# A transformer block with expert routing on one core: new places for every sequence in the hand-made order, and the first weights in another order on two queues

## The chip, the core and the metric

The kernel runs on one core of a Trainium2 chip. A core has TensorE (PE, matrix products; its weight loads are listed as PEld), VectorE (DVE), ScalarE (ACT), GpSimd (POOL) and SyncE (SP, which here only issues DMAs). Each engine takes its instructions in a fixed order; semaphores make one wait for another. The metric is the device time of one execution in microseconds (us); the time before is the median of three runs. A line such as L556 is a line of the kernel file of before. In the changed file the same lines stand lower down by up to 56.

## The reference

Sixteen sequences of 256 tokens with 256 features pass through an attention block with 16 heads of 64, and then through a layer of 8 experts. Each expert takes the 512 tokens that have the highest gate value for it, over all 4096 tokens. All arithmetic is float32. Cut to what matters:

```python
shift = silu(t) @ W_ada.T + b_ada
h = ln(x, ln1_g, ln1_b) + shift
qkv = (h @ Wqkv.T).reshape(b, n, 3, H, HD)
q = ln(qkv[:, :, 0].transpose(0, 2, 1, 3), qn_g, qn_b)
k = ln(qkv[:, :, 1].transpose(0, 2, 1, 3), kn_g, kn_b)
v = qkv[:, :, 2].transpose(0, 2, 1, 3)
attn = softmax(einsum('bhnd,bhmd->bhnm', q, k) / sqrt(HD))
o = einsum('bhnm,bhmd->bhnd', attn, v).transpose(0, 2, 1, 3).reshape(b, n, H * HD)
x = x + o @ Wout.T
tok = x.reshape(-1, d)
gate = softmax(tok @ Wgate.T)
vals, idx = top_k(gate.T, tok.shape[0] // E)
g = ln(tok[idx.T.reshape(-1)], mlp_g, mlp_b).reshape(-1, E, d)
y = gelu(einsum('ked,ehd->keh', g, fc1s) + b1s)
y = einsum('keh,edh->ked', y, fc2s) + b2s
tok = tok.at[idx.T.reshape(-1)].add((y * vals.T[..., None]).reshape(-1, d))
```

## The kernel before

**The work of a sequence.** `First` normalises the two 128-token tiles of x, transposes them (L524) and evicts them with the shift's bias into `hT`. Twelve `Group`s project: groups 0 and 1 are queries, 2 and 3 keys, 4 and 5 values, each for two token tiles t, with 512 columns of the weights `wq`. A query or key group is a chain over the engines: `matmul` (L556, PE), `square` (L569, ACT), `stats` (L573, DVE), `power` (L82, POOL: the inverse root), `scale` (L589, DVE), `transposes` (L598, PE), `evict` (L610, ACT). The mean over a head is taken out by centring the weights once, in place, at the beginning (`center`, L478 to L480). Value groups are only copied (L565) into a tile with the tag `v`.

Four `Quad`s d of four heads each do the attention. A quad has two halves i, and each half two heads j: `scores` (L631, PE), `maxima` (L638, DVE), `exps` (L647, ACT), `invert` (L654, DVE), `normalise` (L658, POOL), `transposes` (L667, PE), `copy` (L675 on DVE or L677 on ACT), `product` (L685, PE), and for the quad as a whole `evict` (L697, DVE) into `oT`. Scores and transposed probabilities share four PSUM tiles with the tag `sc`, projections and most transposes three with `mm`, and the products of a quad, the output projection and the gate share a single one, `po`. Scores use 64 rows of the array for each head, products 64 columns, and all else the full array. `Tail` projects the output (L709), adds x, stores the token, normalises it, and computes the gate (L731, L742).

**Routing and experts.** After the gates of sequences 0 to 14 stand (`Gates`, `Routing.turn`), a search of 30 steps finds each expert's threshold: `compare` (L826, DVE), `count_over` (L856 and L857, PE, result `pc`), `either` and `decide` (DVE). Its steps are strewn among the work of sequence 15. Then the places of the chosen tokens are turned (L912), the token lists of the first experts come from one-hot products (L985, `pls`), tokens are gathered, and sixteen jobs (eight experts, two halves) run up (L1032) and down (L1048) projections. The first matmuls of the experts stand inside the planned order; the rest is a plain loop after it.

**What sets the order.** Every step of the attention is entered in a list with a number, its place, and the list is sorted by place. Engines get their instructions in this order, so a place decides only what stands ahead of what. A steady sequence b has the places of `STEADY` plus b x `PERIOD`. `START` overrides them for the first sequences, `END` for the last ones; `SHIFT` and `CENTER` place the shift and the weights' centring, `GATES`, `TURN`, `SEARCH`, `PLACE`, `LIST`, `UP`, `DOWN` the routing and the first experts. `quad` in the tables has for (d, i) scores, inversion and product, for (d, i, j) the five steps of a head, and `out` has the quads' evictions.

**The first loads.** Before the planned order, SP issues x of sequence 0 (`load_x(0)`), the weights `wa` of the shift, then the groups of `wq` in the order 0, 2, 4, x of sequence 1, 1, 3, 5, and last the output weights `wo`. ACT issues only the small vectors. x of a later sequence is issued by SP 20 places ahead of the sequence's first statistics of tile 0.

Of the kernel before, what the change touches and what calls it, by code (L numbers as in the profile page):

```python
# [18 lines left out]
P = 128  # L19
# [15 lines left out]
GW = 512  # L35
# [8 lines left out]
def kernel(  # L44
# [35 lines left out]
    def rsqrt(dst, src):  # L80
# [59 lines left out]
    PERIOD = 55.74  # L140
    STEADY = dict(
        first=((-86.48, -78.84, -74.84), (-85.13, -84.23, -75.17), (-73.21, -72.54)),
        group={
            (0, 0): (-51.60, -49.66, -48.99, -47.86, -45.60, -40.27, -37.29),
            (0, 1): (-49.89, -47.94, -45.00, -43.96, -42.22, -32.07, -31.41),
            (1, 0): (-24.39, -22.45, -21.77, -20.73, -18.77, -16.60, -15.29),
            (1, 1): (-26.11, -24.16, -23.49, -22.45, -20.71, -11.67, -10.68),
            (2, 0): (-39.83, -37.89, -37.22, -36.18, -34.31, -31.64, -30.60),
            (2, 1): (-38.12, -34.68, -33.12, -32.08, -28.64, -21.80, -20.95),
            (3, 0): (-7.64, -4.23, -3.56, -1.89, 2.62, 3.70, 6.68),  # L150
            (3, 1): (-9.35, -7.41, -6.74, -3.55, -1.19, 9.31, 9.98),
            (4, 0): (-53.91, -51.13),
            (4, 1): (-42.15, -39.94),
            (5, 0): (-11.07, -8.97),
            (5, 1): (-4.61, -2.66),
        },
        quad={
            (0, 0): (0.00, 4.89, 9.75),
            (0, 0, 0): (1.42, 3.71, 5.16, 7.57, 8.23),
            (0, 0, 1): (2.02, 2.81, 6.07, 8.00, 8.67),  # L160
            (0, 1): (-1.04, 3.21, 12.60),
            (0, 1, 0): (0.23, 1.01, 6.97, 8.87, 9.54),
            (0, 1, 1): (0.83, 1.91, 3.48, 8.44, 9.26),
            (1, 0): (10.73, 16.50, 25.41),
            (1, 0, 0): (12.00, 12.78, 17.68, 19.77, 22.02),
            (1, 0, 1): (14.11, 14.89, 16.77, 19.33, 21.66),
            (1, 1): (11.77, 21.34, 28.26),
            (1, 1, 0): (15.91, 19.26, 22.51, 24.97, 25.74),
            (1, 1, 1): (14.71, 20.16, 21.61, 24.53, 25.95),
            (2, 0): (26.39, 30.55, 40.23),  # L170
            (2, 0, 0): (28.29, 29.37, 30.82, 33.50, 35.62),
            (2, 0, 1): (27.69, 28.47, 31.73, 34.37, 35.60),
            (2, 1): (27.43, 36.22, 43.08),
            (2, 1, 0): (29.48, 30.27, 37.58, 39.57, 40.24),
            (2, 1, 1): (28.88, 33.89, 36.67, 38.70, 39.86),
            (3, 0): (41.21, 45.50, 53.71),
            (3, 0, 0): (42.48, 43.26, 46.67, 50.69, 51.36),
            (3, 0, 1): (43.08, 44.16, 45.77, 50.25, 50.92),
            (3, 1): (42.25, 50.11, 56.57),
            (3, 1, 0): (44.90, 45.87, 51.28, 53.28, 53.94),  # L180
            (3, 1, 1): (45.58, 48.93, 50.38, 52.84, 53.67),
        },
        out=(15.31, 30.96, 44.30, 59.03),
        tail=((75.94, 79.63, 83.54, 87.30, 84.99, 86.37, 88.80, 89.54), (90.54, 94.23, 95.33, 101.91, 95.74, 99.41, 105.55, 106.29)),
# [3 lines left out]
            first=((-103.767, -95.871, -91.909), (-97.063, -91.499, -84.828), (-64.982, -60.069)),  # L188
            group={
                (0, 0): (-56.803, -54.747, -51.852, -46.726, -46.286, -40.948, -38.071),  # L190
                (0, 1): (-55.655, -51.889, -46.959, -45.652, -42.360, -35.597, -33.112),
                (1, 0): (-26.197, -24.462, -20.588, -19.209, -14.535, -13.716, -13.269),
                (1, 1): (-32.516, -25.059, -24.852, -21.979, -18.889, -16.671, -15.729),
                (2, 0): (-47.233, -46.547, -44.993, -44.096, -39.234, -33.671, -28.238),
                (2, 1): (-45.275, -40.554, -40.280, -39.778, -36.553, -34.586, -30.446),
                (3, 0): (-12.610, -11.185, -8.404, -8.124, -5.996, 0.834, 3.448),
                (3, 1): (-13.363, -12.739, -11.605, -8.322, -7.543, 0.483, 2.162),
                (4, 0): (-58.243, -54.205),
                (4, 1): (-38.500, -37.978),
                (5, 0): (-9.805, -0.465),  # L200
                (5, 1): (-0.114, 0.811),
            },
            quad={
                (0, 0): (-23.919, -5.908, 12.730),
                (0, 0, 0): (-18.292, -15.414, 1.499, 3.539, 11.030),
                (0, 0, 1): (-14.279, -11.333, -0.174, 4.332, 10.767),
                (0, 1): (-19.036, -1.502, 16.728),
                (0, 1, 0): (-15.547, -8.095, 3.988, 5.433, 14.399),
                (0, 1, 1): (-14.367, -13.775, 4.740, 9.194, 12.898),
                (1, 0): (-9.076, 3.092, 27.287),  # L210
                (1, 0, 0): (-6.911, -0.007, 10.749, 23.221, 26.164),
                (1, 0, 1): (-7.145, 1.038, 18.097, 23.303, 26.927),
                (1, 1): (-5.313, 10.835, 30.672),
                (1, 1, 0): (-5.048, 3.942, 10.903, 21.602, 24.260),
                (1, 1, 1): (-2.237, 6.984, 16.287, 26.090, 28.843),
                (2, 0): (14.616, 29.160, 50.712),
                (2, 0, 0): (18.721, 20.212, 39.985, 46.847, 48.427),
                (2, 0, 1): (17.079, 22.439, 35.099, 36.543, 39.030),
                (2, 1): (14.417, 20.717, 53.224),
                (2, 1, 0): (19.017, 20.432, 39.871, 41.557, 46.931),  # L220
                (2, 1, 1): (16.395, 19.203, 33.057, 36.198, 43.625),
                (3, 0): (28.358, 39.182, 56.816),
                (3, 0, 0): (33.283, 33.907, 42.060, 47.233, 48.706),
                (3, 0, 1): (30.676, 31.677, 45.808, 50.648, 52.914),
                (3, 1): (29.455, 40.685, 56.950),
                (3, 1, 0): (34.034, 35.650, 42.042, 47.065, 52.989),
                (3, 1, 1): (31.817, 31.879, 48.481, 49.433, 55.328),
            },
            out=(21.163, 46.372, 54.377, 59.310),
        ),  # L230
        1: dict(
            first=((-48.940, -38.543, -32.714), (-52.735, -35.719, -31.997), (-29.207, -15.966)),
            group={
                (0, 0): (2.354, 2.737, 3.370, 7.803, 9.249, 18.355, 19.310),
                (0, 1): (4.127, 4.691, 6.834, 9.818, 13.020, 18.898, 22.093),
                (1, 0): (24.336, 28.826, 29.227, 31.339, 32.252, 41.371, 43.504),
                (1, 1): (21.258, 24.606, 28.113, 28.269, 30.764, 34.230, 38.901),
# [7 lines left out]
                (5, 1): (31.404, 35.141),  # L245
            },
        ),
        2: dict(
            first=((6.450, 29.164, 41.308), (24.474, 31.729, 34.174), (50.589, 52.650)),
        ),  # L250
    }
# [1018 lines left out]
```

## Time and profile before

| | us |
|---|---|
| median of 3 runs (1200.65 to 1202.83) | 1201.21 |
| the profiled execution | 1200.95 |
| its span, first to last instruction | 1199.2 |
| L556 projections, 768 records | 357.5 busy, 603 ns each |
| L685 products, 1024 records | 137.7 busy, 391 ns each |
| L667 transposes of the probabilities, 1024 | 136.7 busy, 274 ns each |
| L631 scores, 1024 records | 128.7 busy, 390 ns each |
| L658 normalise on POOL, 512 | 239.9 busy, 489 ns each |
| L647 exps on ACT, 512 | 236.5 busy, 477 ns each |

The first three rows are one execution seen from outside and from inside: what lies between span and time is outside the program's instructions. In a group's row, the busy time is the union of its instructions, and the ns are the length of one. Matmuls are pipelined, so the length of a record is longer than the distance from one start to the next; for what a record costs, starts are to be compared. A float32 matmul leaves two records, a transpose one.

The attention's weights are in within the first 20 us. The expert stage, after about 960 us, keeps PE filled.

### The profile page before, as it was taken

How to read it: one execution, taken by the hardware profiler on the slowest of the kernel's cores; microseconds unless marked ns; L12 is line 12 of the kernel's file. 1: busy time of each engine (PE TensorE's matmuls, PEld its weight loads, DVE VectorE, ACT ScalarE, POOL GpSimd, SP SyncE). 2: the span in 40 equal slices, each digit the busy share in tenths (PEclk: the TensorE clock that was granted, in tenths of full speed). 3: DMA queues.
4: the chain of work that ended last, by engine and by line, in shares of the span. 5: the costliest groups of instructions: out<-in, count | busy, mean ns of one | idle time of the engine just before them, and what ended most of it. 6: DMA issues, size and time to landing. Idle time of an engine off the chain costs nothing. (4 is left out here: it accounts for less than half of the span.)

```text
span 1199.2 us, 19564 instructions
## 1 busy us (share of the span) xinstructions
PE 1169.5 (98%) x6814; PEld 814.2 (68%) x6814; DVE 765.0 (64%) x2274; ACT 618.8 (52%) x1701; POOL 593.5 (49%) x820
## 2 busy tenths in 40 slices
PE   6999999999999999999999999999999899999996
PEld 3566666666675756666666666667755788888885
DVE  7666666657566657666666766665488567865541
ACT  2765565655556655555565655565575233333331
POOL 4564555555454555655555555555574333333332
PEclk9999999999999999999999999999999899999999
DMA  5000000000000000000001000000110366666661
GB/s 186 1 1 5 22 6 23 9 19 10 19 14 14 14 14 27 1 27 5 24 5 31 10 10 10 18 14 15 35 67 2 110 185 184 185 183 183 184 185 23
DMA packets 46738, 62.40 MB, mean 52 GB/s; under 512 B 3888, under 2 KB 39984, under 8 KB 46640
## 3 DMA queue, kind: packets, MB, share of 16 engines
q1 hardware_dynamic: 39808, 52.70, 13.1%
q0 software_dynamic: 6144, 8.39, 3.9%
q8 instruction: 54, 0.88, 0.3%
q14 instruction: 44, 0.36, 0.1%
q10 hardware_dynamic: 688, 0.06, 0.0%
HBM read 48.56 MB, written 12.58 MB: 51 GB/s over the span
## 5 line engine op out<-in xcount | busy, mean ns | idle before, releaser
L658 POOL TENSOR_SCALAR pr<-pr,sums 128x256 f32<-128x256 f32 x512 | 239.9, 489 | 265.1 <-DVE sums L654 252.0
L556 PE MATMUL pm<-wq,hT 128*128 128x512 f32 x768 | 357.5, 603 | 4.2 <-DMA wq<-in_wqkvT 2.7
L647 ACT ACTIVATE pr<-sc,nmax 128x256 f32<-128x256 f32 x512 | 236.5, 477 | 155.3 <-DVE nmax L638 154.8
L82 POOL TENSOR_TENSOR ss<-ss,neghalf 128x8 f32<-128x8 f32 x128 | 210.7, 1650 | 107.0 <-DVE ss L577 98.6
L556 PEld LDWEIGHTS pm<-wq,hT 128*128 128x128 f32 x768 | 137.6, 192 | 145.2 <-issue 134.0
L638 DVE TENSOR_REDUCE nmax<-sc 128x2 f32<-128x512 f32 x256 | 164.8, 681 | 43.4 <-PE sc L631 42.8
L573 DVE TENSOR_REDUCE ss<-sq 128x8 f32<-128x512 f32 x128 | 87.4, 683 | 107.1 <-ACT sq L569 107.0
L667 PEld LDWEIGHTS pp<-ident,pr 128*128 128x128 f32 x1024 | 118.3, 143 | 29.5 <-issue 18.3
L685 PE MATMUL po<-prT,v 128*64 128x256 f32 x1024 | 137.7, 391 | 0.1
L667 PE MATMUL pp<-ident,pr 128*128 128x128 f32 x1024 | 136.7, 274 | 0.0
L631 PE MATMUL sc<-kT,qT 64*128 64x256 f32 x1024 | 128.7, 390 | 0.0
L569 ACT ACTIVATE sq<-pm 128x512 f32<-128x512 f32 x128 | 77.1, 603 | 91.0 <-PE pm L556 89.4
L709 PE MATMUL pw<-wo,oT 128*128 128x256 f32 x512 | 119.1, 386 | 0.0
L1048 PE MATMUL py<-w,hid 128*128 128x256 f32 x512 | 119.0, 385 | 0.0
L1032 PE MATMUL ph<-xT,w 128*128 128x256 f32 x512 | 118.2, 383 | 0.0
L631 PEld LDWEIGHTS sc<-kT,qT 64*128 64x128 f32 x1024 | 93.4, 186 | 34.3 <-issue 23.6
L1058 POOL DMA_INDIRECT out<-y,idx x32 | 51.5, 1611 | 122.2 <-DVE y L1055 61.3
L709 PEld LDWEIGHTS pw<-wo,oT 128*128 128x128 f32 x512 | 96.7, 194 | 14.3 <-issue 1.2
L647 ACT ACTIVATION_READ_ACCUMULATOR pr<-sc,nmax 128x1 f32 x512 | 106.2, 207 | 0.0
L675 DVE COPY prT<-pp 128x512 f32<-128x512 f32 x112 | 76.9, 687 | 45.0 <-PE pp L667 44.7
L1048 PEld LDWEIGHTS py<-w,hid 128*128 128x128 f32 x512 | 96.1, 192 | 13.6
L1039 ACT ACTIVATE hid<-ph,vec 128x256 f32<-128x256 f32 x128 | 60.3, 474 | 85.8 <-PE ph L1032 74.4
(129 smaller groups left out, 1311.8 us busy)
## 6 DMA issues: line engine op xcount, KB each, us to landing
w<-in_fc2T SPq DMA_DIRECT2D x16, 1024.0 KB
w<-in_fc1T SPq DMA_DIRECT2D x16, 1024.0 KB
xs<-in_x SPq DMA_DIRECT2D x16, 256.0 KB
out<-tok SPq DMA_DIRECT2D x32, 128.0 KB
xn_dram<-tn SPq DMA_DIRECT2D x32, 128.0 KB
wq<-in_wqkvT SPq DMA_DIRECT2D x6, 512.0 KB
b<-in_b2s SPq DMA_DIRECT2D x16, 128.0 KB
wo<-in_woutT SPq DMA_DIRECT2D x1, 1024.0 KB
```

Source lines behind the costliest of these rows:

```text
L82: nc.gpsimd.tensor_tensor(dst, src, neghalf[:, : src.shape[1]], ALU.pow)
L556: nc.tensor.matmul(self.pm, hTs[self.b][:, c, bass.ts(self.t, P)], wq[:, c, bass.ts(self.g, GW)], start=(c == 0), stop=(c == DC - 1),)
L573: nc.vector.tensor_reduce(self.ss[:, 0, :], self.sq.rearrange("p (h d) -> p h d", d=HD), AX.X, ALU.add,)
L631: nc.tensor.matmul(self.sc[i, j][:, t, :], qTs[self.b][rows, hp, bass.ts(t, P)], kTs[self.b][rows, hp, :], start=True, stop=True,)
L638: nc.vector.tensor_reduce(self.nmax[i, j], self.sc[i, j], AX.X, ALU.max, negate=True)
L647: nc.scalar.activation(self.pr[i, j][:, t, :], self.sc[i, j][:, t, :], AF.Exp, bias=self.nmax[i, j][:, t : t + 1], scale=1.0, accum_out=se ...
L658: nc.gpsimd.tensor_scalar(self.pr[i, j][:, t, :], self.pr[i, j][:, t, :], self.sums[i][:, 1, j, t : t + 1], 1.0, ALU.mult, ALU.mult,)
L667: nc.tensor.transpose(self.pp[i, j][:, c, bass.ts(t, P)], self.pr[i, j][:, t, bass.ts(c, P)], ident,)
L685: nc.tensor.matmul(self.po[j * HD : (j + 1) * HD, i, :], vs[self.b][:, c, bass.ts(4 * self.d + 2 * i + j, HD)], self.prT[i, j][:, c, :], s ...
L709: nc.tensor.matmul(self.pw, oTs[self.b][:, hp, bass.ts(self.t, P)], wo[:, hp, :], start=(hp == 0), stop=(hp == HP - 1),)
L1032: nc.tensor.matmul(self.ph[f], self.w1[:, c, bass.ts(f, P)], self.xT[:, c, :], start=(c == 0), stop=(c == DC - 1),)
L1048: nc.tensor.matmul(self.py[i], self.hid[:, f, bass.ts(i, P)], self.w2[:, f, :], start=(f == 0), stop=(f == FC - 1),)
```

## The change

Three things change. The tables of places are new throughout: `STEADY` and `PERIOD`, `START`, which now also covers the quads of sequence 1 and the groups of sequence 2, `END`, and all the routing tables. No step is added or left out on PE, DVE, ACT or POOL. The first weights come in the order 4, 0, 2 on SP, and x of sequence 1, weights 1, 3, 5 and `wo` are issued by ACT at a place of their own, `LOADS`. The tag `v` has three buffers instead of two (the experts' first weights use that tag too). x of a later sequence is now issued 20 places ahead of its earliest statistics, whichever tile that is.

The core of the diff; of the tables only parts are shown:

```diff
-    PERIOD = 55.74
+    PERIOD = 55.238
     STEADY = dict(
...
         quad={
-            (0, 0): (0.00, 4.89, 9.75),
...
-            (0, 1): (-1.04, 3.21, 12.60),
...
-            (1, 0): (10.73, 16.50, 25.41),
...
-            (1, 1): (11.77, 21.34, 28.26),
...
+            (0, 0): (0.000, 6.254, 13.508),
...
+            (0, 1): (-1.059, 4.018, 13.509),
...
+            (1, 0): (11.585, 16.798, 31.441),
...
+            (1, 1): (12.644, 23.095, 31.442),
...
+            (2, 0): (29.518, 34.134, 56.102),
...
+            (2, 1): (30.577, 35.467, 56.103),
...
+            (3, 0): (40.264, 45.901, 64.955),
...
+            (3, 1): (41.323, 50.592, 64.956),
...
-        out=(15.31, 30.96, 44.30, 59.03),
+        out=(15.601, 33.534, 58.656, 67.053),
...
-    SHIFT = (-80.440, (-78.087, -69.024), (-69.389, -63.749))
-    CENTER = ((-57.472, -69.391), (-43.212, -34.432), (-52.040, -52.045), (-31.985, -38.697))
+    SHIFT = (-103.533, (-96.272, -72.697), (-98.034, -88.980))
+    CENTER = ((-64.072, -68.386), (-36.649, -27.859), (-57.938, -59.128), (-18.701, -14.089))
+    LOADS = -61.203
...
-        def load_x(b):
+        def load_x(b, queue=nc.sync):
             xs[b] = seq.tile([P, TB, D], F32, tag="xs", bufs=5, name=f"xs{b}")
-            nc.sync.dma_start(
+            queue.dma_start(
                 xs[b], x[b * N : (b + 1) * N, :].rearrange("(t p) d -> p t d", p=P)
             )
...
-        for g in (0, 2, 4, 1, 3, 5):
-            nc.sync.dma_start(wq[:, :, bass.ts(g, GW)], wq_dram[:, :, bass.ts(g, GW)])
-            if g == 4:
-                load_x(1)
-        nc.sync.dma_start(wo, woutT.rearrange("(h p) d -> p h d", p=P))
+
+        def load_wq(g, queue):
+            queue.dma_start(wq[:, :, bass.ts(g, GW)], wq_dram[:, :, bass.ts(g, GW)])
+
+        for g in (4, 0, 2):
+            load_wq(g, nc.sync)
+
+        def later_loads():
+            load_x(1, nc.scalar)
+            for g in (1, 3, 5):
+                load_wq(g, nc.scalar)
+            nc.scalar.dma_start(wo, woutT.rearrange("(h p) d -> p h d", p=P))
...
             if b not in tiles:
-                tiles[b] = seq.tile(shape, F32, tag=tag, name=f"{tag}{b}")
+                tiles[b] = seq.tile(
+                    shape, F32, tag=tag, bufs=3 if tag == "v" else 2, name=f"{tag}{b}"
+                )
...
-                self.w1 = seq.tile([P, DC, DD], F32, tag="v", name="w1")
+                self.w1 = seq.tile([P, DC, DD], F32, tag="v", bufs=3, name="w1")
...
+        at([LOADS], later_loads)
...
             if b > 1:
-                at([its["first"][0][0] - 20.0], partial(load_x, b))
+                at([min(its["first"][t][0] for t in range(TB)) - 20.0], partial(load_x, b))
```

In the steady tables the second number of a half's scores, inversion and product triple is the inversion and the third the product: the two products of a quad now have adjoining places (13.508 and 13.509), where before they were apart (9.75 and 12.60) with the next quad's scores (10.73 and 11.77) between them.

## The prediction

> **What bounds the kernel now.** I read the page first, then the stages in equal windows, then who TensorE (PE) waited for, then PE's timeline in three places: a steady sequence, the first 46 us, and the stage between the last attention sequence and the experts.
>
> ```profile
> span 1199.2 us, 19564 instructions
> ...
> PE 1169.5 (98%) x6814; PEld 814.2 (68%) x6814; DVE 765.0 (64%) x2274; ACT 618.8 (52%) x1701; POOL 593.5 (49%) x820
> ...
> PE   6999999999999999999999999999999899999996
> ```
>
> PE is busy 98% of the span; the others have a third or more to spare. PE's idle time sits in the first slice, in the few slices near 900 us, and in the last one (after the last matmul only the final scatter is under way). The stages say the same, in us:
>
> ```profile
> 0.00:30.00 30.00, 19.31 (x46) 9.18 (x47) 21.86 (x53) 6.67 (x11) 13.77 (x27) 0.94 0.57 186
> ...
> 860.00:900.00 40.00, 37.20 (x206) 24.15 (x204) 31.42 (x128) 22.43 (x62) 27.36 (x35) 1.00 0.20 70
> 900.00:940.00 40.00, 36.17 (x252) 24.77 (x253) 33.03 (x162) 16.09 (x46) 18.89 (x34) 0.91 0.03 8
> 940.00:960.00 20.00, 18.27 (x106) 15.58 (x103) 10.68 (x53) 6.92 (x13) 5.00 (x5) 0.91 0.47 154
> ```
>
> The columns are length, busy PE, PE weight loads, VectorE (DVE), ScalarE (ACT), GpSimd (POOL), granted clock, DMA share, GB/s. One whole steady sequence looks like this:
>
> ```profile
> 186.18:242.37 56.19, 56.19 (x321) 36.78 (x320) 36.51 (x82) 32.50 (x94) 30.29 (x45) 1.00 0.05 15
> ```
>
> A sequence takes 56.19 us, all of it PE work; the next ones have the same length to 0.01 us. No wait is left there, so only less PE time per sequence can shorten it. That less is possible is seen in the run lengths of the steady timeline (start, length, x records; a float32 matmul is two records):
>
> ```profile
> 413.01 1.08 PE L685 MATMUL po<-prT,v 128*64 128x256 f32 x8
> 414.02 2.00 PE L631 MATMUL sc<-kT,qT 64*128 64x256 f32 x16
> 415.95 1.08 PE L685 MATMUL po<-prT,v 128*64 128x256 f32 x8
> 416.96 0.66 PE L598 MATMUL pq<-ident,qk 128*128 128x128 f32 x4
> ```
>
> ```profile
> 87.73 1.95 PE L685 MATMUL po<-prT,v 128*64 128x256 f32 x16
> 89.61 2.00 PE L631 MATMUL sc<-kT,qT 64*128 64x256 f32 x16
> ```
>
> From start to start, eight product records take 414.02 - 413.01 = 1.01 us, but sixteen in one run take 89.61 - 87.73 = 1.88, not 2.03. Each run of products so carries 0.147 us that is no streaming (unrounded starts), and each run of scores about 0.20.
>
> The start, and the stage before the experts:
>
> ```profile
> 11.06 9.51 PE L556 MATMUL pm<-wq,hT 128*128 128x512 f32 x16 [2.70 <-DMA wq<-in_wqkvT]
> ```
>
> ```profile
> 37.77 0.63 PE L598 MATMUL pq<-ident,qk 128*128 128x128 f32 x4 [0.81 <-DVE qk L589]
> ```
>
> ```profile
> 893.26 0.16 PE L857 MATMUL pc<-cnt,twice 128*128 128x1 bf16 x1 [0.33 <-DVE reach L826]
> ...
> 931.10 0.19 PE L985 MATMUL pls<-give,oh 128*128 128x10 bf16 x1 [0.50 <-POOL oh L976]
> ...
> 932.30 7.13 PE L709 MATMUL pw<-wo,oT 128*128 128x256 f32 x20
> ```
>
> The first projection waits for its weights; the search for the gate threshold and the one-hot lists leave PE short waits; and after them twenty records of L709 take 7.13 us, 0.35 each instead of 0.215 in the steady part: PE runs cold.
>
> **What the Trainium skill says.** "TensorEngine Tiling (Array Packing)", Key Properties: changing the tiling mode drains TensorE. Scores use half the rows, products half the columns, all else the full array, and the trace agrees with 0.09 to 0.10 us at each change. "TensorE: Matmul & The Clock Gate", Part 1: PE starts at half clock and needs a sustained window of some 3.4 us. The trace agrees: projection records at 11.06 follow at 0.85 us and from about 15.5 us on at 0.43. "DMA: Bandwidth & Descriptors", Issuing engines are not separate DMA queues: two issuing engines share the same 16 DMA engines and save only issue time. So the second queue is no extra bandwidth; before shows 186 GB/s over the first 30 us from one queue, and no two loading queues.
>
> **Part 1, steady places.** The numbers are only sort keys: they set each engine's order. In the order of the changed program the two products of a quad stand together and lie beside scores or other work; before, each quad's scores were flanked by two short product runs. Per sequence, product runs fall from 8 to 4, scores stay at 4 runs: 4 x 0.147 = 0.59 us. The new sequence is 56.19 - 0.59 = 55.60. Over the whole attention, product runs fall from 123 to 64 and score runs rise from 67 to 69: 59 x 0.147 - 2 x 0.20 = 8.3 us less PE work. Instruction counts are otherwise equal.
>
> What could take this back is a wait. The tightest new one: products of quad 3, scores of the next sequence, products of its quad 0 now follow each other, and both products use the single bank "po". Between them DVE must copy the first out (680 ns for the 128x512 copy at L697). The scores in between give 1.93 + 0.1 us; with 0.1 us of signalling each way the copy needs 0.88, so about 1.1 us is spare. In DVE's order two prT copies stand ahead of it, whose sources are done before the products start. I take 0.
>
> The third buffer of "v" is what lets the next sequence's values be written earlier (L565); nothing else waits on it. The experts' first weights share that tag, but stand on SP's queue behind second weights that keep two buffers, so the experts do not load earlier: 0.
>
> **Part 2, the beginning.** Group 4's weights needed no centring and were used first, but landed third, at 11.06. Now they are first; the first weights landed by 7.5 before (L478 began at 7.54 without a wait for them). What is late next is hT: before, its bias (L459) stood on DVE behind a centring of 1.6 us and came at 9.06. Now it stands ahead, at 7.6 to 8.1; the transposes end at 8.36, two ACT evictions of about 0.5 follow, and the first projection can start at 9.05: 2.0 us earlier. Group 0's weights land second, by about 9.3; centring 2 x 1.55 ends at 12.4, just when the cold group 4 ends (4 x 0.855 from 9.05), so it costs nothing. Group 2 lands third, 11.06, centred by 15.5, needed at 16.8. ACT's five issues (x1, three weights, wo; ACT's issues took 0.44 to 0.52 each) stand behind the hT evictions, 9.5 to 12; ACT's next work, the first square, is due at 15.2, so they are hidden. Their 2.75 MB at the 340 to 400 GB/s seen at 8 to 16 us are in by about 20; the first user (centring of group 1) comes after that.
>
> From there I walked the four engine queues with the durations of before. The chain square, reduce, power, scale before the fourth projection stays 4.06 us long and moves with the start. The first scores come at about 32.2 instead of 34.96; transposes of sequence 1 (0.44) were moved behind them; the wait of 0.81 at 37.77 shrinks to about 0.45; the second quad's scores come at 40.3 instead of 45.70 with 2.6 us less PE work done by then. Net gain 2.9 us. Sequence 1 starts later than before, so there is less filler while the softmax of sequence 0 runs; my walk shows no wait up to the first probability transposes (about 45) and ends there. Bounds: nothing gained at all if later waits eat it, 5 us if the cold stretch at 26 to 29 us goes too. I take -2.9.
>
> **Part 3, the end.** The search still has 30 steps in PE's order, about 28.4 us of other PE work between them before and 29.0 after. But steps with only one transpose block (0.44 us) between them rise from 10 to 15. Such a step takes 1.06 us (893.26 to 894.32), some 0.45 of it idle: +2.2 us. Between the turned places and the first list matmul stand 4.6 us instead of 3.6: -1.0; before the second gathered tile 7.5 instead of 7.1: -0.4; a few small fillers -0.2. Sum +0.6. Bounds: -3 if PE no longer goes cold after the lists (20 x 0.135 = 2.7), +4 if it goes cold in the search too. The last expert stage and its final scatter are untouched.
>
> **Sum**, against the profiled execution: it took 1200.95 us, span 1199.2. -8.3 - 2.9 + 0.6 = -10.6 gives 1190.35; its own time lies 0.26 below the median 1201.21 of the runs. I predict 1190.4.
>
> **The rivals.** (a) The start gives its lead back: with sequence 1 begun later, PE runs dry between 45 and 130 us. Sum -8.3 + 0.6: 1193.3. For it: later filler; against: PE had no wait from 42 us on before, with the same engines. (b) The end also gains, with a warmer PE: -8.3 - 2.9 - 3 gives 1187.0. (c) Slower: the "po" copy. If DVE reaches it three operations (2.04 us) late, PE loses 2.04 - 1.1 = 0.94 in each of some 13 sequences, 12 us, which is where it turns the sign; four operations late, 1.62 x 13 = 21, 1211. For it: it recurs each period, and DVE is busy 36.5 of 56.2 us; against: 1.1 us spare and nothing ahead of it that waits for these scores. (d) The shorter runs are not real (time follows the slowest engine, not PE): PE at 56.19 of 56.19 speaks against it; about 1200.
>
> **How the numbers follow.** Forecast 0.66, (a) 0.17, (b) 0.08, (c) 0.06, (d) 0.03. (a) and (b) lie inside the range: start +-3, end -3.6 to +3.4, steady 0 to +2 give 1184.5 to 1196.5, which leaves out (c), (d) and a tail. About 0.2% (2.4 us) is what a measurement of this kernel can tell: faster 0.92, within it 0.02, slower 0.06.
>
> **What would show it.** Right: steady sequences of 55.6 us with PE busy throughout; first projection near 9 us; second quad's scores near 40; some 13 us of waits and cold clock near the lists as before. Wrong: any "po from DVE oT" wait that comes back each sequence; PE idle between 45 and 130 us; a period at or above 56.2; PE cold through the search.

## The result, and the profile after

| | before | after |
|---|---|---|
| median of 5 runs, us | 1201.21 (1200.65 to 1202.83) | 1194.45 (1193.64 to 1195.09) |
| the profiled execution | 1200.95 | 1194.45 |
| its span | 1199.2 | 1192.6 |

The ratio is 0.9945, with a 95% interval of 0.9931 to 0.9958: 6.8 us faster. The forecast was 1190.4; the measured time lies 4.0 us above it. The page of after begins as that of before did:

```profile
span 1192.6 us, 19612 instructions
...
PE 1162.9 (98%) x6814; PEld 817.1 (69%) x6814; DVE 760.9 (64%) x2274; ACT 624.5 (52%) x1701; POOL 590.7 (50%) x820
...
PE   7999999999999999999999999999998989999996
```

TensorE (PE) is busy for 6.6 us less (1169.5 to 1162.9) and is as full as it was. In the 33rd of the 40 slices (954 to 984 us) there is now a notch that before did not have. The steady sequence, by windows (length, busy PE, PEld, DVE, ACT, POOL, granted clock as a share of full speed, DMA share, GB/s):

```profile
297.81:353.50 55.69, 55.69 (x322) 36.96 (x321) 36.19 (x82) 32.99 (x95) 30.17 (x45) 1.00 0.05 15
```

It is 55.69 us instead of 56.19, still without a gap. In PE's timeline (start, length, name, x records) the products now come in runs of sixteen records:

```profile
419.20 1.95 PE L740 MATMUL po<-prT,v 128*64 128x256 f32 x16
...
428.22 1.95 PE L740 MATMUL po<-prT,v 128*64 128x256 f32 x16
430.09 2.00 PE L686 MATMUL sc<-kT,qT 64*128 64x256 f32 x16
432.02 1.95 PE L740 MATMUL po<-prT,v 128*64 128x256 f32 x16
```

L740 is L685 of before, L686 is L631. No product waits for the copy of the bank "po". The first projection (L611, formerly L556) answers to the one at 11.06 of before:

```profile
9.02 9.20 PE L611 MATMUL pm<-wq,hT 128*128 128x512 f32 x16 [0.66 <-ACT hT L585]
...
23.54 3.62 PE L611 MATMUL pm<-wq,hT 128*128 128x512 f32 x4 [0.87 <-ACT qT L665]
```

It starts 2.0 us earlier and waits for hT, not for weights. Four records at 23.54 take 3.62 us, twice their usual 1.9: the clock is at half there.

The windows at the end, in the columns above:

```profile
900.00:940.00 40.00, 35.30 (x243) 26.13 (x239) 31.67 (x156) 15.76 (x38) 17.46 (x29) 0.91 0.23 76
940.00:960.00 20.00, 20.00 (x125) 17.66 (x125) 9.64 (x48) 7.26 (x13) 3.91 (x5) 1.00 0.43 133
960.00:980.00 20.00, 16.55 (x100) 13.63 (x99) 10.91 (x59) 4.80 (x10) 7.68 (x9) 0.91 0.55 158
```

Between 960 and 980 PE is idle for 3.45 us and then runs at a lower clock. Before, nothing of that kind was there:

```profile
960.00:980.00 20.00, 20.00 (x129) 17.28 (x128) 12.97 (x66) 9.17 (x17) 8.08 (x10) 1.00 0.66 191
```

Three marks in PE's timeline cut the profiled executions into stretches: the turned gates (the transposition with which the search's stage begins), the first list product, and the first up-projection of job 2. Jobs are counted from 0; early finish and late finish are two of the experiments below.

| us from the span's start | before | after | early finish | late finish |
|---|---|---|---|---|
| turned gates | 876.69 | 865.70 | 866.72 | 876.98 |
| first list product | 927.77 | 920.10 | 919.62 | 928.05 |
| job 2's first up-projection | 975.37 | 968.56 | 963.05 | 981.62 |
| end | 1199.23 | 1192.65 | 1187.00 | 1206.23 |

Up to the turned gates after gains 10.99 us. From there to job 2 it loses 4.18 (98.68 becomes 102.86). The stretches hold the same PE records but for eight records of scores, which after has behind the turned gates and before had ahead of them. At half a run of sixteen (1.93 us from start to start) they are about 1.0 us, so for equal work after gains about 10.0 and then loses about 3.2. The last stretch is the same to 0.2. So what is missing was lost in the 100 us around the lists, and this is where the experiments went.

**How that loss looks.** Job 0's result leaves in two scatters that add to the output, one for each half of its tokens, on GpSimd's queue. Job 2's gather stands behind the second scatter in that queue. The timeline of before, GpSimd's lines and one of SP's queue (start, length, engine, line, operation; in brackets the idle time before it and what ended it):

```profile
957.28 1.66 POOL L1058 DMA_INDIRECT out<-y,idx  x1 [11.34 <-DVE gates L748]
960.06 0.38 SPq L948 DMA_DIRECT2D w<-in_fc2T  x1
962.24 1.57 POOL L1058 DMA_INDIRECT out<-y,idx  x1 [3.30 <-issue]
```

The first scatter (L1058) leaves 2.8 us ahead of the load of job 2's weights on SP (2 MB, freed by job 0's last down-projection), and the second follows after a pause of 3.3 us. The same place after:

```profile
947.96 0.38 SPq L1003 DMA_DIRECT2D w<-in_fc2T  x1
949.07 1.67 POOL L1113 DMA_INDIRECT out<-y,idx  x1 [11.43 <-DVE y L1110]
957.61 1.57 POOL L1113 DMA_INDIRECT out<-y,idx  x1 [6.87 <-DMA out<-y,idx]
960.71 1.05 POOL L1059 DMA_INDIRECT xg<-xn_dram,idx  x1
...
963.77 0.30 PE L1068 MATMUL px<-ident,xg 128*128 128x128 f32 x1 [2.57 <-DMA xg<-xn_dram,idx]
...
965.34 3.43 PE L1103 MATMUL py<-w,hid 128*128 128x256 f32 x8
```

Now the load is 1.1 us ahead. The first scatter lands 7.8 us after its start (3.9 in before), at 956.83, just after the last of the 2 MB (956.60). The second scatter waits 6.87 us for that, the gather (L1059) follows only at 960.71, PE waits 2.57 us and once more 0.88 for the gathered tokens, and the eight records behind that take 3.43 us instead of 1.89. The scatter is late because the places `DOWN` of the new tables put VectorE's finish (bias and gate weight, L1109 and L1110) of the half whose down-projection is done first (i = 1, at about 944.0) behind that of the other half (done at about 947.9). Before, the half done first was finished first. The two bias additions, before and then after:

```profile
956.17 0.43 DVE L1054 TENSOR_TENSOR y<-py,b 128x256 f32<-128x256 f32 x1 [2.81 <-PE py L1048]
960.07 0.43 DVE L1054 TENSOR_TENSOR y<-py,b 128x256 f32<-128x256 f32 x1 [3.01 <-PE py L1048]
```

```profile
947.96 0.42 DVE L1109 TENSOR_TENSOR y<-py,b 128x256 f32<-128x256 f32 x1 [1.28 <-PE py L1103]
948.69 0.42 DVE L1109 TENSOR_TENSOR y<-py,b 128x256 f32<-128x256 f32 x1
```

### The profile page after: what moved, and what is told of

Same layout as the page of the kernel before. It is cut to its first block, busy times and chain, and to the rows that moved or that the text cites. A ratio compares the mean times of both kernels' runs of the same rounds, so it can differ in the third digit from the quotient of the medians.

```text
span 1192.6 us, 19612 instructions
## 1 busy us (share of the span) xinstructions
PE 1162.9 (98%) x6814; PEld 817.1 (69%) x6814; DVE 760.9 (64%) x2274; ACT 624.5 (52%) x1701; POOL 590.7 (50%) x820
## 5 line engine op out<-in xcount | busy, mean ns | idle before, releaser
L611 PE MATMUL pm<-wq,hT 128*128 128x512 f32 x768 | 365.3, 606 | 2.2 <-ACT qT L665 0.9
L713 POOL TENSOR_SCALAR pr<-pr,sums 128x256 f32<-128x256 f32 x512 | 236.8, 481 | 208.9 <-DVE sums L709 162.2
L611 PEld LDWEIGHTS pm<-wq,hT 128*128 128x128 f32 x768 | 134.9, 192 | 126.3 <-issue 112.2
L722 PE MATMUL pp<-ident,pr 128*128 128x128 f32 x1024 | 139.2, 273 | 0.2
L686 PE MATMUL sc<-kT,qT 64*128 64x256 f32 x1024 | 129.2, 390 | 0.0
L740 PE MATMUL po<-prT,v 128*64 128x256 f32 x1024 | 126.7, 389 | 0.0
L686 PEld LDWEIGHTS sc<-kT,qT 64*128 64x128 f32 x1024 | 93.2, 186 | 40.6 <-issue 30.4
L1087 PEld LDWEIGHTS ph<-xT,w 128*128 128x128 f32 x512 | 95.3, 191 | 13.4
```

The source lines that it names most:

```text
L611: nc.tensor.matmul(self.pm, hTs[self.b][:, c, bass.ts(self.t, P)], wq[:, c, bass.ts(self.g, GW)], start=(c == 0), stop=(c == DC - 1),)
L686: nc.tensor.matmul(self.sc[i, j][:, t, :], qTs[self.b][rows, hp, bass.ts(t, P)], kTs[self.b][rows, hp, :], start=True, stop=True,)
L713: nc.gpsimd.tensor_scalar(self.pr[i, j][:, t, :], self.pr[i, j][:, t, :], self.sums[i][:, 1, j, t : t + 1], 1.0, ALU.mult, ALU.mult,)
L722: nc.tensor.transpose(self.pp[i, j][:, c, bass.ts(t, P)], self.pr[i, j][:, t, bass.ts(c, P)], ident,)
L740: nc.tensor.matmul(self.po[j * HD : (j + 1) * HD, i, :], vs[self.b][:, c, bass.ts(4 * self.d + 2 * i + j, HD)], self.prT[i, j][:, c, :], s ...
L1087: nc.tensor.matmul(self.ph[f], self.w1[:, c, bass.ts(f, P)], self.xT[:, c, :], start=(c == 0), stop=(c == DC - 1),)
```

## The experiments

Every kernel was run four times or more beside the kernel before, on the same chip as it. The first two rows are the sitting of the result; the experiments come from three other sittings, each on a chip of its own, in which before had medians of 1200.87, 1200.17 and 1200.47 and single times from 1195.28 to 1203.03. The changed kernel was not run again in them, so a difference of medians between it and an experiment can be off by about 1 us, and the ratios to before are the safer comparison. The last two columns are from each kernel's single profiled execution: the time lost because the clock was granted at less than full (5 us times one minus the clock, summed over windows of 5 us, from 15 us to the last matmul), and the span less that loss. A comparison of the last column is called "at equal clock" below.

| kernel | median (lowest to highest) | ratio to before (95%) | lost | span less loss |
|---|---|---|---|---|
| before | 1201.21 (1200.65 to 1202.83) | 1 | 6.8 | 1192.4 |
| after | 1194.45 (1193.64 to 1195.09) | 0.9945 (0.9931 to 0.9958) | 6.9 | 1185.8 |
| split products | 1198.69 (1196.27 to 1199.99) | 0.9983 (0.9974 to 0.9991) | 5.1 | 1190.2 |
| one queue | 1195.31 (1192.70 to 1195.56) | 0.9953 (0.9939 to 0.9968) | 5.1 | 1185.8 |
| old first order | 1196.80 (1192.12 to 1197.37) | 0.9955 (0.9938 to 0.9972) | 3.4 | 1187.7 |
| old start | 1197.70 (1195.98 to 1199.99) | 0.9981 (0.9971 to 0.9991) | 8.6 | 1188.6 |
| old end | 1194.18 (1191.56 to 1197.19) | 0.9944 (0.9927 to 0.9961) | 8.6 | 1183.7 |
| old both | 1196.83 (1192.92 to 1199.69) | 0.9967 (0.9952 to 0.9982) | 6.9 | 1189.2 |
| early finish | 1188.96 (1186.15 to 1190.07) | 0.9897 (0.9877 to 0.9916) | 3.4 | 1183.6 |
| late load | 1187.97 (1186.26 to 1190.36) | 0.9897 (0.9882 to 0.9912) | 5.1 | 1183.0 |
| late finish (in before) | 1206.95 (1203.62 to 1208.62) | 1.0050 (1.0035 to 1.0065) | 8.6 | 1197.7 |
| early projections | 1199.15 (1197.03 to 1200.25) | 0.9993 (0.9984 to 1.0002) | 10.3 | 1186.6 |
| warm search | 1195.10 (1191.54 to 1196.49) | 0.9956 (0.9941 to 0.9971) | 3.4 | 1186.2 |
| early finish, warm lists | 1187.35 (1184.73 to 1187.84) | 0.9884 (0.9868 to 0.9900) | 3.4 | 1182.5 |

The losses are 2, 3, 4, 5 or 6 times 1.7 us. The last section comes back to this.

### Is it the product runs? Split products

The change's steady order, with the two products of quads 1 and 2 drawn apart again: 86 product runs instead of 64.

```diff
-            (1, 0): (11.585, 16.798, 31.441),
+            (1, 0): (11.585, 16.798, 29.450),
...
-            (2, 0): (29.518, 34.134, 56.102),
+            (2, 0): (29.518, 34.134, 54.100),
```

> The changed kernel with two of the four steady product pairs taken apart again, so that in each steady sequence two score runs are flanked by short product runs as before (86 product runs in the whole instead of 64). Theory 'mode changes': each further run costs 0.147 us, so the steady period goes from 55.69 to about 55.98 us and the whole is 22 x 0.147 = 3.2 us slower than the changed kernel (about 1197.7). Rival 'the period is set by something else, the shorter period came from other places': the period stays at 55.69 and the time at 1194.5.

```profile
408.73 0.60 PE L577 MATMUL ph<-ident,xn 128*128 128x128 f32 x4
464.72 0.60 PE L577 MATMUL ph<-ident,xn 128*128 128x128 f32 x4
```

The period is 55.99 (464.72 less 408.73), 0.30 us more than in the changed kernel, for two more runs in it: 0.15 us each, as the prediction read it from the starts of before. The median is 4.2 us above the changed kernel's, where 3.2 were expected; the further 1 us is no more than the comparison of medians can be off. The shorter steady sequence is due to the product runs, and rival (d), that they are not real, falls.

### Is it the second queue? One queue, and the old first order

One queue: all first loads on SP, in the new order; ACT issues none of them.

```diff
         for g in (4, 0, 2):
             load_wq(g, nc.sync)
+        load_x(1)
+        for g in (1, 3, 5):
+            load_wq(g, nc.sync)
+        nc.sync.dma_start(wo, woutT.rearrange("(h p) d -> p h d", p=P))
...
-        at([LOADS], later_loads)
```

> The changed kernel with all first loads on SP, in the order 4, 0, 2, x1, 1, 3, 5, wo; nothing on ACT. Theory 'order of the weights, not the queue': first projection near 9.0 us again and the time within 1 us of the changed kernel. Rival 'the second queue brings the data sooner or keeps the first weights free of company': the second and third weights land later, first scores later than 31.9 us, up to 2 us slower.

Old first order: the groups come as 0, 2, 4 on SP again, and the rest stays on ACT.

```diff
-        for g in (4, 0, 2):
+        for g in (0, 2, 4):
```

> The changed kernel with the first weights on SP in the old order 0, 2, 4; the rest stays on ACT. Theory 'order of the weights': group 4 lands third again, the first projection waits for it until about 11.0 us, and the time grows by the 2.0 us of lead (about 1196.5). Rival 'the lead came from the bias standing ahead of the centring': first projection stays near 9 to 10 us and the time grows by less than 1 us.

The first projection, with one queue and with the old order:

```profile
9.02 8.67 PE L610 MATMUL pm<-wq,hT 128*128 128x512 f32 x16 [0.66 <-ACT hT L584]
```

```profile
10.94 8.78 PE L611 MATMUL pm<-wq,hT 128*128 128x512 f32 x16 [2.57 <-DMA wq<-in_wqkvT]
```

With one queue the first projection starts at 9.02 as in the changed kernel, and the span less its loss of clock is the same, 1185.8. With the old order it starts at 10.94 after a wait of 2.57 us for its weights, and the span so corrected is 1.9 longer. So the order of the three loads makes the earlier beginning, and nothing shows for the second queue. The times alone could not tell this: the runs of the old order lie near 1192.5 (three) and near 1197 (four), about 4 us apart, and its ratio to before (0.9955) lies within the changed kernel's interval.

### The parts alone: old start, old end, old both

Old start has `START`, `SHIFT`, `CENTER` and the first loads of before in the changed kernel; old end has `END`, the search and all routing tables of before, moved by the difference of 13 periods; old both has both, and so only the new steady order.

> The changed kernel with the start, the first loads and the filling transposes of the kernel before, and the new steady order and new end. If the start's gain of 2.9 us was real, this run is 2.5 to 3 us slower than the changed kernel: 1197 to 1197.5. If the lead of the start is given back in the first whole sequence, it is 1194.5. The steady period should be 55.69 us as in the changed kernel.

> The changed kernel with the ordering of the end, the search and the routing of the kernel before (its planned times shifted by the shorter period), and the new steady order and new start. If the miss lies wholly in the end, this run has the start and steady gains of 10.9 us at the last tile and loses nothing after it: 1201.2 - 10.9 = about 1190 to 1190.5. If the end was in truth neutral, it gives 1194.5 like the changed kernel.

> The changed kernel with the start, loads and filling transposes and the end, search and routing of the kernel before: the new steady order alone. The parts should add up at equal clock: in the single executions, with the time lost to half clock after the first 15 us taken off each, old start is 2.9 above the changed kernel and old end 2.0 below it, so this one should have a span of about 1186.6 to 1187 so corrected, and by the clock between 1190 and 1195 as it ran. If the steady order brought the 8.3 us by itself, it is 1192.9 or less in the median; if it brought only what the period shows (0.50 us in about 12 periods), about 1195.

Old start is 3.2 us above the changed kernel in the median, 4.3 by the ratios (0.9981 and 0.9945) and 2.8 at equal clock: the start is worth about what was forecast (2.9), or somewhat more. The lead is not given back, so rival (a) falls.

Old end missed its expectation in the median (1194.18, not 1190), and is hard to read. The new steady order and the old end do not fit together: PE waits 0.84 us for VectorE's qk at 734.94 and 0.38 for ACT's v at 759.87, which neither full kernel does (from start to start, three steps there take 1.9 us more than their like elsewhere); the old end has 73 product runs and 68 score runs in the whole where the changed kernel has 64 and 69, by the prediction's prices about 1.1 us more; and the clock fell in the midst of the search. At equal clock it is nevertheless 2 us better than the changed kernel. That points to the new end, but it is the experiments of the next part that settle it.

Old both is 3.6 us below before in the median. The period alone would give about 0.50 x 12 = 6.0; 1.9 of that is taken back at the same joint, which old both has too. At equal clock it came to 1189.2 instead of the expected 1186.6 to 1187; 1.3 of the difference is seen (its first weights were waited for 3.8 us, those of old start 2.5), and the rest stays open.

### The finish of job 0: early finish, late load, late finish

Early finish: the changed kernel with the finish of the first-done half back where its down-projection ends.

```diff
-    DOWN = ((1056.315, 1057.008), (1047.604, 1057.278))
+    DOWN = ((1056.315, 1057.278), (1047.604, 1049.900))
```

> The changed kernel with the first expert's second half finished and scattered as soon as its down projection is done (DOWN's second entry from 1057.278 to 1049.900), as the kernel before had it. Theory 'the late scatter collides with the next weights': its scatter leaves at about 946 us instead of 949, ahead of the weights' load at 948, the second scatter no longer waits 6.9 us, the gather of the third job comes on time, and PE's waits of 3.7 us at 961 to 965 fall to under 1: 3 us faster (about 1191.5). Rival 'the gather is late for another reason (the load itself)': the wait at the third job's transposes stays above 2.5 us and the time within 1 us of the changed kernel.

The timeline, as above:

```profile
945.70 1.67 POOL L1113 DMA_INDIRECT out<-y,idx  x1 [8.29 <-DVE y L1110]
947.75 0.38 SPq L1003 DMA_DIRECT2D w<-in_fc2T  x1
950.46 1.57 POOL L1113 DMA_INDIRECT out<-y,idx  x1 [3.09 <-DMA out<-y,idx]
...
960.85 0.64 PE L1068 MATMUL px<-ident,xg 128*128 128x128 f32 x4
```

The scatter is 2.0 us ahead of the load, the second waits 3.09 us for it instead of 6.87, and job 2's transposes wait for nothing. The run is 5.5 us faster than the changed kernel in the median, more than expected: 3.45 us of waiting are gone, and with them the stretch at half clock behind the wait, another 1.7. Between the marks of the table, from the first list product to job 2, it is 48.46 against 43.43 us.

This moves two things at once, the finish and its order against the load. Late load keeps the finish as late as the change has it and moves the load: job 2's weights are issued on ACT's queue behind the third activation of job 1.

```diff
-        jobs[2].load()
...
                     a.gelu(s)
+                    if k == 1 and s == 2:
+                        jobs[2].load(nc.scalar)
```

> The changed kernel with one thing altered in the experts: the 2 MB of weights of job 2 are not issued on SP as soon as job 0's last down-projection frees their buffer, but on ScalarE's queue behind job 1's third activation (about 951 us), so behind the first scatter of job 0, which leaves at 949.07. The finish of job 0 keeps its place, so that scatter is as late as in the changed kernel. If the load in front of the scatter is what holds the second scatter for 6.9 us, that wait falls to about 3, job 2's gather goes at about 956 to 957, TensorE's wait of 2.6 + 1.1 us at job 2's transposes goes, the clock stays full there, and the run comes to about 1189 to 1191. If the late finish alone is the cause, the wait stays and the run is within 1 us of 1194.45.

```profile
950.01 1.67 POOL L1112 DMA_INDIRECT out<-y,idx  x1 [11.59 <-DVE y L1109]
951.62 0.37 ACTq L1002 DMA_DIRECT2D w<-in_fc2T  x1
954.71 1.60 POOL L1112 DMA_INDIRECT out<-y,idx  x1 [3.03 <-DVE chunk L1012]
```

The scatter leaves even later than in the changed kernel, but the load is behind it, and the second scatter follows after 3.03 us. The median is 1187.97. So the late finish alone costs nothing that shows: it costs because it lets 2 MB of weights go ahead. The load changed its queue here as well as its time; but early finish, with the load still on SP, has the same pause of 3 us, so who is ahead is enough.

Late finish puts the order of the change into the kernel before, and nothing else:

```diff
-    DOWN = ((1020.447, 1020.575), (1014.649, 1019.361))
+    DOWN = ((1020.447, 1020.575), (1014.649, 1020.625))
```

> The kernel before with one planned time altered: the finish of job 0's first half (the two VectorE operations whose result the first scatter carries) goes behind that of the second half, as in the changed kernel. If this order is what costs the time, the first scatter leaves 4 us later and behind the weights' load (957.3 becomes about 961, the load is at 960.1), the second waits 7 us for it, and job 2's transposes wait: 3 to 5.5 us slower, 1204 to 1206.5. If the order matters only together with the rest of the new end, it stays at 1201.

```profile
959.08 0.38 SPq L948 DMA_DIRECT2D w<-in_fc2T  x1
960.20 1.66 POOL L1058 DMA_INDIRECT out<-y,idx  x1 [15.19 <-DVE y L1055]
970.26 1.57 POOL L1058 DMA_INDIRECT out<-y,idx  x1 [8.41 <-DVE cand L845]
```

The load is 1.1 us ahead again, the second scatter comes 8.41 us after the first, PE waits 4.00 us for job 2's tokens (up to 976.33), and the median is 6.5 us above that of before beside it (ratio 1.0050, 1.0035 to 1.0065), somewhat more than expected. Taken out of one kernel and put into the other, the same order moves the median by 5.5 and 6.5 us.

The fourteen profiles agree without exception. In eight of them the load is about 1.1 us ahead of the first scatter (after, split products, one queue, old first order, old start, late finish, early projections, warm search): the second scatter then waits 6.8 to 8.4 us, and one or two stretches at half clock follow between 960 and 985 us. In the other six the scatter is 1.6 to 2.8 us ahead: the pause is 2.9 to 3.3 us, and no such stretch follows. So this fall of the clock comes with the wait and is not one of chance. In all fourteen the second scatter leaves 0.8 or 1.1 us after the first has landed, also where the bracket names another instruction that ended about then, as in late load and late finish.

### The waits at the lists: early projections, warm search, warm lists

Early projections: twelve records of output projections that stand behind the first list are put ahead of the piece of it that waits for GpSimd's one-hots (the rows of zeros and ones from which the lists are made).

```diff
-    EARLY = {14: (894.209, 902.691,), 15: (1025.834, 1032.355,)}
+    EARLY = {14: (894.209, 902.691,), 15: (1025.834, 1026.500,)}
```

> One planned time of the changed kernel is altered: the six token projections of the last tile's second half (12 records, 2.6 us of TensorE work) go ahead of the piece of the lists that waits for GpSimd's one-hots. If the end lost time because the piece in front of the first list has nothing left to fill TensorE's wait for those one-hots, the piece from the search's last transposition to the first list shrinks by 1 to 2.6 us and the run comes to about 1192 to 1193.5 us. If that wait is set by GpSimd alone and something else is late next (the index lists, the gather), the list chunk starts at the same time and the run stays within 0.5 us of the changed kernel's 1194.45.

```profile
920.39 2.84 PE L764 MATMUL pw<-wo,oT 128*128 128x256 f32 x12
...
928.24 0.69 PE L786 MATMUL pg<-ident,tok 128*128 128x128 f32 x2 [2.35 <-DVE tok L771]
...
933.09 0.90 PE L1068 MATMUL px<-ident,xg 128*128 128x128 f32 x3 [3.95 <-DMA xg<-xn_dram,idx]
```

A miss: 4.7 us slower. The waits for the one-hots are filled, but the list is done at the same time (GpSimd sets it), and the gather that follows now has only eight projection records over it instead of twenty. It is waited for 3.95 us, the sum of the last tokens (x and the projected output) 2.35 us, and two more stretches at half clock follow. The filler had been where it was needed.

Warm search: three more transposes of the identity, into columns that nobody reads, in each of the last six steps of the search. They are added work; nothing is left out.

```diff
-                self.pc = ps.tile([P, 1], F32, tag="mm", bufs=3, name="pc")
+                fill = 3 if n < 6 else 0
+                whole = ps.tile([P, P * (fill > 0) + 1], F32, tag="mm", bufs=3, name="pc")
+                self.pc = whole[:, :1]
+                for _ in range(fill):
+                    nc.tensor.transpose(whole[:, 1 : P + 1], ident, ident)
```

> Each of the last six steps of the search gets three more transposes of the identity into columns that nobody reads, so that TensorE is busy in the gaps. If the one-block fillers of the changed kernel let the clock fall in the search's tail, the group po x16 after the search takes about 1.95 us instead of 3.46, the piece after it about 0.5 us less, and the run about 2 us less: 1192.5. If the fall of the clock there is a matter of chance from run to run and not of the fillers, the time spreads as that of the changed kernel does, about 1194.5; if the extra blocks push the steps apart it is up to 2 us more.

No gain: 1195.10. In its profile the product group after the search does take 1.95 us; but so it does in early finish, late load, old first order, one queue and split products, which have no such filler. Of the nine kernels with the new search and no filler, four show the stretch at half clock there. Its coming and going is not due to the fillers.

Warm lists: early finish, and four such transposes ahead of each of the five list products that wait for the one-hots.

```diff
                 for t in range(a, min(b, self.tiles)):
+                    if self is jobs[0] and 10 <= t < 15:
+                        idle = ps.tile([P, P], F32, tag="mm", bufs=3, name="idle")
+                        for _ in range(4):
+                            nc.tensor.transpose(idle, ident, ident)
```

> Early finish of job 0, and four transposes of the identity into unread columns ahead of each of the five list matmuls that wait for GpSimd's one-hots, so that TensorE is not idle there. If those waits are what lets the clock fall for the 3.4 us after the lists, that stretch goes and the run is 1.7 us below early_finish's 1188.96: about 1187. If the clock falls there for another reason, or the five groups delay the lists, it stays at 1189 or goes up to 1190.5.

The windows of early finish, and of early finish with warm lists:

```profile
920.00:925.00 5.00, 2.37 (x24) 1.83 (x24) 3.61 (x22) 0.00 (x0) 3.65 (x6) 0.81 0.02 3
925.00:930.00 5.00, 5.00 (x24) 4.24 (x23) 4.90 (x27) 0.00 (x0) 1.89 (x2) 0.85 0.19 54
```

```profile
920.00:925.00 5.00, 4.77 (x56) 3.85 (x56) 3.33 (x21) 0.00 (x0) 3.68 (x7) 1.00 0.02 3
925.00:930.00 5.00, 4.69 (x32) 3.90 (x30) 4.90 (x28) 0.16 (x1) 2.12 (x2) 1.00 0.21 60
```

With PE kept busy over the waits (2.37 to 4.77 us of 5) the clock stays full, and the twenty records after the lists take 4.56 us instead of 5.88. The other thirteen profiles all lose 1.7 us or more right after the lists (between 920 and 940 us; early projections behind its longer waits), and this one nothing. Its total loss is 3.4 all the same, because the stretch at 910 us, which early finish has not, is there. The median, 1187.35, lies 1.6 below early finish and close to the expected 1187, but the two intervals overlap, so the gain rests on the traces more than on the times. It is the lowest median of all, 13 us below before; early finish and late load beat both kernels too. Late load together with warm lists was not tried.

## Why the prediction was right, and where it was short

**Part 1 and part 2 together: right in kind, a little too large.** 8.3 + 2.9 = 11.2 us were forecast, and the profile shows 10.99 up to the turned gates. That they lie so close is luck, because about 1.0 of the 10.99 is work moved behind the mark. The gain of a period was sized too large: 0.50 us where 0.59 were forecast, with no wait in the sequence. Scaled by that, 8.3 becomes about 7.0, and 7.0 + 2.9 = 9.9 fits the 10.0 for equal work (an estimate from these figures). The price of a product run is not what was off (split products: 0.15); where the 0.09 goes is open. The start was sized right: first projection 9.02 (9.05 forecast), first scores 31.90 (32.2), wait 0.38 (0.45), second quad's scores 39.98 (40.3), and no wait from 45 to 130 us.

**"I take 0" for the copy of "po": right.** No product waits for it in any sequence; rival (c) falls.

**The third buffer of "v" and the second queue.** No gain was claimed for either. One queue bears this out for the queue; the buffer was not tried alone.

**Part 3, the end: the failed term.** "+0.6" measured +4.18 from the turned gates to job 2, about +3.2 for equal work, and +0.2 after. Three of its terms were off:

- The search's short steps were priced at +2.2. The search grew by 0.67 (40.14 to 40.81 from its first to its last step), and about 0.5 of that is work moved into it (the eight score records, less four transposes of 0.11 us each). The short steps cost next to nothing.
- The fillers ahead of the first list and ahead of the second gather were to give 1.4. The stretch from the search's last step to the first list instead grew by 2.66 (8.78 to 11.44). The four transposes are 0.44 of it. About 1.5 is the clock: PE ran at half clock there, and in early finish, with the same order but a full clock there, the stretch took 9.93. A cold search was the bound of +4 that I had named and not taken.
- The term that weighs most was not in the sum at all. I wrote that the last expert stage is untouched, and counted the fillers between the lists from PE's order alone; I did not look at the order of the two finishes on VectorE, nor at what stands behind the scatter on GpSimd's queue and beside it on SP's. That order is worth 5.5 us in the changed kernel and 6.5 in the kernel before.

That no more than 4 us were missing is in part luck: the order of the finishes took about 5 us from the stretch between the lists and job 2, and other parts of the new end gave about 4 back, most of it clock, which the prediction had only as a bound. With the order of the finishes left as it was, the changed kernel would have been at 1188.96, below the forecast, since some of the end did gain. From the first list product to job 2 before took 47.60 us, after 48.46 and early finish 43.43. Of the 4.2 us between before and early finish 3.4 are clock (before lost 3.4 us after the lists and 1.7 behind its wait at 949, early finish 1.7 after the lists), and the shorter wait for job 1's gather (0.37 us in early finish, 0.32 in after, 1.56 in before) covers the rest. Nor do the bounds of the three parts add up to the stated range of 1184.5 to 1196.5: their plain sum is 1183.8 to 1198.8.

**Rivals (a) and (b).** The result lies near rival (a)'s 1193.3, but for another reason: the start kept its lead. Rival (b), an end that gains with a warmer PE (1187.0), did not happen in after; early finish (1188.96) and warm lists (1187.35) come near it.

## What to carry to other kernels

When places change, read the order of every queue, not only that of the bound engine: a pair of vector instructions that swap costs nothing where they stand, but here it put a scatter behind a bulk load, and behind the scatter stood the next gather. Ask of each transfer with a successor what large transfer may be ahead of it. And before a filler is moved to a wait, see which wait it covers now.

## What was not expected of the hardware

After a scatter of 128 rows of 1 KB the next one leaves about 3 us after the first's issue has ended when the first left 1.6 to 2.8 us ahead of a 2 MB load, and 6.8 to 8.4 us when the load was about 1.1 us ahead. In seven of those eight profiles the first scatter lands within 0.3 us of the last of the 2 MB (in late finish 1.5 us after it). The load was on SP's queue in all eight; a load on ACT's queue ahead of the scatter was not tried. What holds the scatter back inside the DMA engines, these runs do not show.

The clock falls in whole stretches, and each costs about 1.7 us. In the profile of after, in windows of 5 us:

```profile
910.00:915.00 5.00, 4.75 (x28) 2.64 (x26) 3.21 (x10) 1.27 (x3) 0.57 (x2) 0.66 0.01 3
...
965.00:970.00 5.00, 5.00 (x18) 4.06 (x19) 1.16 (x5) 1.20 (x3) 0.10 (x1) 0.66 0.26 34
```

A clock of 0.66 over 5 us is 3.4 us at half and the rest at full, 1.7 us lost. The Trainium skill, "TensorE: Matmul & The Clock Gate", Part 1, says that the clock is either half or full and is decided in windows of some 3.4 us that run freely and are not reset when a kernel starts; the losses in the table, all close to multiples of 1.7, agree. Such windows would explain why the same short waits cost a stretch in one profile and none in another (the stretch near 25 us is there in after and missing in one queue, old first order and warm search), and why the times of one kernel lie some 2 or 4 us apart; no experiment here moved the windows, so this part is not shown. With effects of 2 us to be told, the span less this loss was the better measure; but single starts still differ by about 1 us with the landing of the first weights.
